# Layer-norm of the second and third token block done channels first, between the evictions of the query/key/value stage

## The chip, the cores and the metric

The kernel runs on one core of a Trainium2 chip. The metric is the device time of one execution in microseconds; the runs before the change have a median of 2848.19. A core has five engines that work side by side, each through its own queue in order: TensorE (PE in the profile; its weight loads are PEld), VectorE (DVE), ScalarE (ACT), GpSimd (POOL) and SyncE (SP), which here issues nearly all DMA transfers. Matmul results stand in PSUM banks until VectorE or ScalarE copies them out, which is called an eviction.

## The reference

The input is an image of 48 x 48 tokens with 768 channels, in fp32. Layer 0 is a transformer block: layer-norm of each token, queries, keys and values from one weight matrix, attention over all 2304 tokens with 12 heads and relative positions in two directions, a projection, a second layer-norm and an MLP with GELU. Layer 1 mixes frequencies: a two-dimensional FFT, a small two-layer network on blocks of 96 channels, an inverse FFT, and the input added. The change touches only the beginning:

```
mu = jnp.mean(x, axis=-1, keepdims=True)
var = jnp.var(x, axis=-1, keepdims=True)
xn = (x - mu) * jax.lax.rsqrt(var + LN_EPS) * g + b
qkv = xn.reshape(B, H * W, C) @ qkv_w + qkv_b
```

## The kernel before

The query/key/value stage takes the tokens in three blocks of 768. TensorE multiplies over the partition axis, so the normalised tokens must stand channels first: `xt`, six chunks of 128 channels by 768 tokens. A block is worked off in nine *units*: six `queries_and_keys` (each for 128 channels of the queries and 128 of the keys) and three `values` (each for two groups of 128 tokens). The order of units is written out in `orders`: block one has the six pairs and then the three values, block two the three values first, block three one pair, the values, five pairs.

A unit is a two-by-two Strassen scheme, so it has seven products instead of eight (`seven`, line 420). A product is three matmuls of 128x128 by 128x384 in fp32, and the profile records each matmul twice. The scheme needs sums of weights and sums of tokens. The sums of weights are made by GpSimd: `left` (lines 159 to 162), for each pair in `weights_of` and once for the values in `weights_of_values`. The sums of tokens are made by VectorE: `sums_of_tokens` (line 177), four operations of 1152 elements for a block; the last one works in place. The seven products go to four PSUM banks, m0 to m3, in the order m0, m1, m2, m3, m0, m2, m3. ScalarE copies the first (line 429), VectorE makes `u` and `u7` of the second and third (431, 433), and four outputs `o` are evicted (460 and 462, or 490 and 492 for values) and stored by SP from seven buffers. A bank is written again only after it has been read.

The tokens of a block come with two `arrive` calls of three tiles of 128 tokens, tokens first. `normal` normalises a tile in place: two `bn_stats`, one `bn_aggr`, a square root on ScalarE, a reciprocal, and one operation of 128x768 (lines 119 to 129). At the beginning of a block `channels_first` turns the six tiles: 36 transposes on TensorE (line 408), into the same banks m0 to m3, evicted with gain and offset by VectorE (411) and ScalarE (415), each six times. Then `sums_of_tokens`, then the first unit. Blocks share one `xt` and one `xs`, in the buffer `main`, and so a block can be turned only when the block before has been multiplied.

Weights of a pair have two slots; after a unit has used a slot, `weights_of` loads the weights for the unit after the next one, and GpSimd makes their sums.

What sets the order: TensorE and SP run in the order of the code (`tc.manual_schedule`, line 545). In this stage the queues of VectorE, ScalarE and GpSimd are ordered by a scheduler, which may, for instance, put the statistics of a tile between two evictions. From the attention on VectorE and ScalarE follow the code too. The buffer `shared` (8064 columns) holds the first head pair's queries, keys and values from block three on; before that it only takes the raw selection constants. After the last unit the relative positions `relative(0, 2)` use TensorE (294), ScalarE (238, 239) and VectorE (240), and then the attention begins with scores (562).

Of the kernel before, what the change touches and what calls it, by code (L numbers as in the profile page):

```python
# [46 lines left out]
def block_then_afno(  # L47
# [3 lines left out]
    x_blocks,  # L51
    qkv_w,
# [50 lines left out]
    oT = dram.tile([C, T], F32, name="oT")  # L103
    den_d = dram.tile([NC * (T // G), 2 * G], F32, name="den_d")
# [88 lines left out]
    with ExitStack() as flag_scope:  # L193
# [12 lines left out]
        with ExitStack() as att:  # L206
# [110 lines left out]
            def constants():  # L317
                nc.vector.memset(relT, 0.0)
                for j in range(2):
                    nc.sync.dma_start(out=relT[ts(j, 64), j], in_=rel)  # L320
                nc.vector.tensor_scalar(relT, relT, HD**0.5, None, ALU.mult)
                raw = shared[:, ds(3 * T + 2 * G, 2 * P)].rearrange("p (a k) -> p a k", a=2)
                for j in range(2):
                    nc.sync.dma_start(out=raw[ts(j, 64)], in_=c_select)
                nc.vector.tensor_copy(select, raw)

            def queries_keys_values(qkv):
# [14 lines left out]
                xt, xs = view(NC, TB), view(3, 3, G)  # L342
# [58 lines left out]

                def channels_first(g):
                    x3 = arrived[g]
# [35 lines left out]
                def queries_and_keys(p, pr, w, ws):  # L439
                    b11, b21, t3, b22, t1, t2, t4 = parts_of_tokens(xt, xs)  # L440
# [15 lines left out]
                    for i, j, bank, other in seven(product):  # L456
# [8 lines left out]
                        )  # L465

                def values(p, i):

                    b11, b21, t3, b22, t1, t2, t4 = parts_of_tokens(xt, xs, ts(i, P))
# [17 lines left out]
                    for k, j, bank, other in seven(product):  # L487
# [6 lines left out]
                        nc.sync.dma_start(out=v_d[ts(t, P), ts(k - 1, CH)], in_=o)  # L494

# [18 lines left out]
                for p in range(T // TB):  # L514
                    for g in (2 * p, 2 * p + 1):
                        channels_first(g)
                    sums_of_tokens(xt, xs)
                    for n, (kind, i) in enumerate(orders[p]):
                        if kind:
                            values(p, i)  # L520
                        else:
                            queries_and_keys(p, i, *ahead.pop(0))
                            if pairs_left:
                                ahead.append(weights_of(pairs_left.pop(0), slot % 2))
                                slot += 1

                        if p == 0 and n in (3, 4):
                            weights_of_values(n - 3)
                        elif (p, n) == (0, 5):
                            constants()  # L530
                        elif p < 2 and n in (1, 2):
                            arrive(2 * p + 1 + n)
                        if p < 2 and 2 <= n < 8:
                            normal(6 * p + 4 + n)
# [7 lines left out]
                        elif p == 2 and n == 5:  # L542
                            fetch_values(0)

# [1175 lines left out]
```

## Time and profile before

| what | value |
|---|---|
| median of three runs | 2848.19 us (2845.54 to 2848.93) |
| the profiled execution, its own time | 2846.82 us |
| its span, first to last instruction | 2844.9 us |
| TensorE busy in the span | 2794.3 us, 98% |
| first product of block one | 21.25 us |
| transposes of block two, of block three begin | 147.13 us, 275.29 us |
| first score product of the attention | 418.75 us |
| granted TensorE clock | 0.999 |

In the lines of a profile a name such as L408 is a line of the kernel, `out<-in` names what an instruction writes and reads, `x18` says how many equal instructions stand together, and what is in brackets is the idle time of the engine before it and the instruction that ended it. In the timeline the first two numbers are start and length in microseconds. SPq is the queue of DMA issues. A group of instructions has its sum and the mean of one in nanoseconds.

### The profile page before, as it was taken

The page shows a single profiled execution, that of the slowest core. Times are in us where ns is not written, and L with a number is a line of the kernel's source. Part 1 is how long each engine was busy: PE and PEld are TensorE (multiplying, and loading weights), DVE is VectorE, ACT ScalarE, POOL GpSimd, SP SyncE. Part 2 cuts the span into 40 slices and gives each one's busy share as a digit, 9 for nine tenths or more (in the row PEclk, how much of TensorE's full clock was granted, in tenths as well). Part 3 has the DMA queues.
Part 4 walks back from the last instruction along what each step waited for, and adds up shares of the span by engine and source line. Part 5 has one row for each costly group of instructions (what it writes and reads, how often), then busy time and mean ns, then how long its engine had stood idle before and what let it go on. Part 6 is the DMA issues. An engine that isn't in the chain of part 4 may idle for free. (4 is left out here: it accounts for less than half of the span.)

```text
span 2844.9 us, 41192 instructions
## 1 busy us (share of the span) xinstructions
PE 2794.3 (98%) x15829; PEld 1722.6 (61%) x15829; DVE 1699.3 (60%) x2540; ACT 920.4 (32%) x1474; POOL 643.5 (23%) x650
## 2 busy tenths in 40 slices
PE   8999999999999999999999999999999999999998
PEld 4555655656566656565555555555555555556887
DVE  5343327676767676666656766675565565566666
ACT  1011116656566566665601211031011211102332
POOL 2303110000000000000064333432333422322433
PEclk9999999999999999999999999999999999999999
DMA  4423275374573736545242121121121212123254
GB/s 146 136 100 111 92 163 110 62 134 83 82 141 54 133 63 110 123 69 97 78 178 78 50 67 45 66 96 51 53 67 45 100 56 67 45 65 112 62 160 143
DMA packets 216493, 262.78 MB, mean 92 GB/s; under 512 B 24524, under 2 KB 196908, under 8 KB 214752
## 3 DMA queue, kind: packets, MB, share of 16 engines
q1 hardware_dynamic: 213784, 258.03, 36.6%
q8 instruction: 127, 2.08, 0.3%
q10 hardware_dynamic: 2440, 1.84, 0.2%
q14 instruction: 78, 0.64, 0.1%
q0 software_dynamic: 64, 0.20, 0.0%
HBM read 143.96 MB, written 52.31 MB: 69 GB/s over the span
## 5 line engine op out<-in xcount | busy, mean ns | idle before, releaser
L581 ACT ACTIVATE main<-sp 128x768 f32<-128x768 f32 x648 | 516.5, 812 | 34.0 <-PE sp L571 19.3
L725 DVE TENSOR_TENSOR pairs<-pairs,main 128x1536 f32<-128x1536 f32 x252 | 443.1, 1758 | 27.2 <-DVE pairs L725 0.9
L571 PE MATMUL sp<-terms,select 64*128 64x384 f32 x1296 | 412.2, 629 | 0.0
L1245 DVE TENSOR_TENSOR main<-o,main 128x384 f32<-128x384 f32 x540 | 299.0, 556 | 38.5 <-PE o L1243 0.3
L1183 PE MATMUL h<-shared,w 128*128 128x384 f32 x864 | 296.6, 486 | 0.7 <-POOL w2s L165 0.7
L562 PE MATMUL sp<-shared 64*128 64x384 f32 x1296 | 265.3, 485 | 2.8 <-DVE o L462 2.2
L562 PE MATMUL sp<-qT,kT 64*128 64x384 f32 x1296 | 264.0, 484 | 0.0
L451 PE MATMUL m<-main 128*128 128x384 f32 x756 | 246.3, 487 | 3.2 <-DVE main L177 2.6
L1183 PEld LDWEIGHTS h<-shared,w 128*128 128x128 f32 x864 | 163.9, 190 | 116.2 <-POOL w2s L165 1.3
L1183 PE MATMUL h<-shared,w1s 128*128 128x384 f32 x648 | 226.7, 486 | 0.0
L627 POOL TENSOR_TENSOR inverse<-inverse,rden 24x32 f32<-24x32 f32 x36 | 15.2, 421 | 927.1 <-DVE sums L626 836.5
L594 PE MATMUL op<-main,shared 128*64 128x384 f32 x1296 | 217.4, 488 | 0.0
L1189 ACT ACTIVATE hT<-c,vec 128x384 f32<-128x384 f32 x108 | 66.5, 615 | 464.5 <-DVE c L1195 464.5
L594 PE MATMUL op<-main,v 128*64 128x384 f32 x1296 | 216.4, 488 | 0.0
L725 DVE TENSOR_TENSOR pairs<-main 128x1536 f32<-128x1536 f32 x36 | 63.3, 1758 | 247.1 <-ACT main L581 247.1
L451 PEld LDWEIGHTS m<-main 128*128 128x128 f32 x756 | 143.1, 190 | 104.0 <-issue 4.9
L1195 DVE TENSOR_TENSOR c<-h,u 128x384 f32<-128x384 f32 x108 | 60.2, 557 | 212.4 <-PE h L1183 212.4
L1243 PE MATMUL o<-w2s,hs 128*128 128x384 f32 x432 | 174.9, 487 | 2.0 <-DVE hs L160 2.0
L1243 PE MATMUL o<-w,hT 128*128 128x384 f32 x432 | 174.9, 486 | 1.9 <-DVE mv L123 1.5
L571 PEld LDWEIGHTS sp<-terms,select 64*128 64x128 f32 x1296 | 125.5, 186 | 83.6
L1183 PEld LDWEIGHTS h<-shared,w1s 128*128 128x128 f32 x648 | 123.1, 190 | 85.9
L165 POOL TENSOR_TENSOR w2s<-w 128x384 f32<-128x384 f32 x36 | 36.0, 1000 | 566.2 <-DMA w<-in_mlp_w_dram 350.1
(187 smaller groups left out, 3995.2 us busy)
## 6 DMA issues: line engine op xcount, KB each, us to landing
w<-in_mlp_w_dram SPq DMA_DIRECT2D x72, 768.0 KB
terms<-col_parts SPq DMA_DIRECT2D x432, 72.0 KB
terms<-row_hi SPq DMA_DIRECT2D x216, 72.0 KB
terms<-row_lo SPq DMA_DIRECT2D x216, 72.0 KB
main<-in_qkv_w_dram SPq DMA_DIRECT2D x36, 384.0 KB
z<-zt SPq DMA_DIRECT2D x48, 192.0 KB
x<-in_x_blocks_dram SPq DMA_DIRECT2D x18, 384.0 KB
k_d<-o SPq DMA_DIRECT2D x36, 192.0 KB
```

The costliest lines, as they stand in the source:

```text
L165: eng.tensor_tensor(t[0], b12, b11, ALU.subtract)
L451: nc.tensor.matmul(bank, a[:, c, :], b[:, c, :], start=(first and c == 0), stop=(c == 2), skip_group_check=not first,)
L562: nc.tensor.matmul(sp[:, j, :G], kT[at, ts(kt, P)], qT[at, ts(c, G)], start=first, stop=not first,)
L571: nc.tensor.matmul(sp[:, j, :G], select[at, a % 2], ready[pr, c][at, a // 2, b], start=first, stop=not first,)
L581: nc.scalar.activation(p, sp[:, :, :G], AF.Exp, scale=HD**-0.5)
L594: nc.tensor.matmul(op[ts(j, 64)], v[:, kt, ts(j, 64)], exps[:, kt, j, :], start=(kt == 0), stop=(kt == NT - 1),)
L725: nc.vector.tensor_tensor(pairs, so_far, exps[:, ds(kt - 1, 2)], ALU.add)
L1183: nc.tensor.matmul(bank[i], a[:, c, :], b[:, c, :], start=(start and c == 0), stop=(c == 2), skip_group_check=not start,)
L1189: nc.scalar.activation(h[:, i, ts(k, G)], src, AF.Gelu, bias=col(V_B1 + 2 * n + i))
L1195: nc.vector.tensor_tensor(t, src, other, ALU.add)
L1243: nc.tensor.matmul(bank[k], a, b, start=start, stop=True, skip_group_check=not start)
L1245: nc.vector.tensor_tensor(dst, bank[k], dst, ALU.add)
```

## The change

The tokens of blocks two and three get to `xt` in another way. They are still loaded tokens first, but only to measure them: `measured` makes mean and variance of a tile, three tiles after the third and three after the fourth unit of the block before. `gathered` makes the reciprocal standard deviation of all six tiles at once, `written` turns the twelve columns of statistics with one transpose into rows and writes them to DRAM, and `spread_out` reads them back into all 128 partitions. The same tokens are loaded a second time channels first (`brought`, from a new input `x_turned`, which is laid out on the host like the others). Then, in the units six to nine of the block before, one small operation after each of the four output evictions (`next_hook`) normalises the new block: `centred` on GpSimd subtracts the mean of a chunk of 128 channels, `scaled` on VectorE multiplies by gain and reciprocal deviation, with the offset added on ScalarE, and `token_sum` makes the four sums of tokens in the ninth unit.

Block two stands in `shared` (`apart`), blocks one and three in `main`. Block one is done as before. From the first unit to the end of the stage VectorE, ScalarE and GpSimd now follow the order of the code too (`part_by_part`). The weights of the values are loaded one unit earlier, and `constants` is split in two steps.

```diff
@@ queries_keys_values @@
-                xt, xs = view(NC, TB), view(3, 3, G)
+                apart = xt, xs
+                tokens = [(view(NC, TB), view(3, 3, G)), apart]
+                tokens.append(tokens[0])
...
+                def gathered(p):
+                    st = ln1.tile([P, 2, 6], F32, name="st", bufs=2)
+                    nc.scalar.activation(st[:, 1], stats[p][:, 1], AF.Sqrt, bias=eps)
+                    nc.vector.reciprocal(st[:, 1], st[:, 1])
+                    nc.vector.tensor_copy(st[:, 0], stats[p][:, 0])
+                    stats[p] = st
+                def written(p):
+                    bank = small_bank()
+                    nc.tensor.transpose(
+                        bank[:12, :P], stats[p].rearrange("p k t -> p (k t)"), ident
+                    )
+                    rows = ln1.tile([12, P], F32, name="stat_rows", bufs=1)
+                    nc.scalar.copy(rows, bank[:12, :P])
+                    nc.sync.dma_start(out=stat_d[p], in_=rows)
+                def measured(t):
+                    p, i = divmod(t, 6)
...
+                    for k in range(2):
+                        nc.vector.bn_stats(parts[:, k, :], src[:, ts(k, C // 2)])
+                    nc.vector.bn_aggr(stats[p][:, :, i], parts.rearrange("p a b -> p (a b)"))
+                def brought(p):
+                    for i in range(2):
+                        nc.sync.dma_start(
+                            out=tokens[p][0][:, ds(3 * i, 3)],
+                            in_=x_turned[ds(i * CH, CH), ts(p, TB)].rearrange(
+                                "(c p) t -> p c t", p=P
+                            ),
+                        )
+                def spread_out(p):
+                    spread[p] = ln1.tile([P, 2, TB], F32, name="stat_all", bufs=1)
+                    nc.sync.dma_start(
+                        out=spread[p].rearrange("p k t -> p (k t)"),
+                        in_=stat_d[p].rearrange("k t -> (k t)").partition_broadcast(P),
+                    )
+                def centred(p, c):
+                    a = tokens[p][0][:, c]
+                    nc.gpsimd.tensor_tensor(a, a, spread[p][:, 0], ALU.subtract)
+                def scaled(p, c):
+                    a = tokens[p][0][:, c]
+                    nc.vector.scalar_tensor_tensor(
+                        a, a, col(V_LN1G + c), spread[p][:, 1], ALU.mult, ALU.mult
+                    )
+                    nc.scalar.activation(a, a, AF.Identity, bias=col(V_LN1B + c))
+                def token_sum(p, i):
...
+                    nc.vector.tensor_tensor(dst, a, b, ALU.subtract)
+                hooks = []
+                def next_hook():
+                    if hooks:
+                        hooks.pop(0)()
@@ queries_and_keys, values: after the store of each output o @@
+                        next_hook()
@@ the loop over blocks @@
-                    for g in (2 * p, 2 * p + 1):
-                        channels_first(g)
-                    sums_of_tokens(xt, xs)
+                    if p == 0:
+                        for g in range(2):
+                            channels_first(g)
+                        sums_of_tokens(*tokens[0])
+                    part_by_part = ExitStack()
+                    part_by_part.enter_context(
+                        tc.manual_schedule(
+                            engines={
+                                mybir.EngineType.DVE, mybir.EngineType.Activation,
+                                mybir.EngineType.Pool,
+                            }
+                        )
+                    )
                     for n, (kind, i) in enumerate(orders[p]):
+                        if p < 2:
+                            q = p + 1
+                            if n in (5, 6):
+                                hooks += [partial(centred, q, 3 * (n - 5) + c) for c in range(3)]
+                            if n in (6, 7):
+                                hooks[:0] = [partial(scaled, q, 3 * (n - 6) + c) for c in range(3)]
+                            if n == 8:
+                                hooks += [partial(token_sum, q, j) for j in range(4)]
...
+                        while hooks:
+                            next_hook()
-                        if p == 0 and n in (3, 4):
-                            weights_of_values(n - 3)
-                        elif (p, n) == (0, 5):
-                            constants()
-                        elif p < 2 and n in (1, 2):
+                        if p < 2 and n in (1, 2):
                             arrive(2 * p + 1 + n)
-                        if p < 2 and 2 <= n < 8:
-                            normal(6 * p + 4 + n)
+                        if p == 0 and n in (2, 3):
+                            weights_of_values(n - 2)
+                        elif p == 0 and n in (5, 6):
+                            constants(n - 5)
+                        if p < 2 and n in (2, 3):
+                            for t in range(3):
+                                measured(6 * (p + 1) + 3 * (n - 2) + t)
+                            if n == 3:
+                                gathered(p + 1)
+                        elif p < 2 and n == 4:
+                            brought(p + 1)
+                            written(p + 1)
+                            spread_out(p + 1)
```

## The prediction

> **What bounds the kernel now.** I read the page's first part, then TensorE's timeline over the query/key/value stage (0 to 419 us) and its waits there, then what the other engines and the DMA queue do at the places found.
>
> ```profile
> PE 2794.3 (98%) x15829; PEld 1722.6 (61%) x15829; DVE 1699.3 (60%) x2540; ACT 920.4 (32%) x1474; POOL 643.5 (23%) x650
> ```
>
> TensorE sets the end: in the page's chain of waits it has 44%, no other engine more than 2%. So the change is worth what it takes off TensorE's own queue between 0 and 419 us, less what it makes TensorE wait. The timeline (start, length, engine, line, operation, count):
>
> ```profile
> 104.63 2.10 PE L482 MATMUL m<-wv,main 128*128 128x384 f32 x6
> 107.69 2.20 PE L482 MATMUL m<-wvs,main 128*128 128x384 f32 x6 [0.95 <-POOL wvs L160]
> 110.26 2.20 PE L482 MATMUL m<-wv,main 128*128 128x384 f32 x6 [0.38 <-POOL wv L162]
> ...
> 118.11 2.10 PE L482 MATMUL m<-wvs,main 128*128 128x384 f32 x6
> 120.04 2.10 PE L482 MATMUL m<-wv,main 128*128 128x384 f32 x6
> ...
> 147.13 2.28 PE L408 MATMUL m<-ident,x 128*128 128x128 f32 x18
> 149.85 2.19 PE L408 MATMUL m<-ident,x 128*128 128x128 f32 x18 [0.44 <-DVE main L411]
> 152.49 2.20 PE L482 MATMUL m<-wv,main 128*128 128x384 f32 x6 [0.44 <-DVE main L411]
> 155.21 2.20 PE L482 MATMUL m<-wvs,main 128*128 128x384 f32 x6 [0.52 <-DVE main L177]
> 157.25 2.10 PE L482 MATMUL m<-wv,main 128*128 128x384 f32 x6
> ```
>
> A product (six records) takes 1.935 us from start to start (118.11 to 120.04), a unit of seven 13.55. Three losses show: a first value unit of 15.41 (104.63 to 120.04), waiting for GpSimd's weight sums; 36 transposes between blocks; and a second product late for the token sums (L177). The later part of the same view:
>
> ```profile
> 275.29 2.33 PE L408 MATMUL m<-ident,x 128*128 128x128 f32 x18
> ...
> 280.70 2.20 PE L451 MATMUL m<-main 128*128 128x384 f32 x6 [0.44 <-DVE main L411]
> 284.13 11.94 PE L451 MATMUL m<-main 128*128 128x384 f32 x36 [1.22 <-DVE main L177]
> 295.91 2.10 PE L482 MATMUL m<-wv,main 128*128 128x384 f32 x6
> ...
> 418.75 0.88 PE L562 MATMUL sp<-shared 64*128 64x384 f32 x3 [2.17 <-DVE o L462]
> ```
>
> The last line is attention's first product. All engines just before it:
>
> ```profile
> 417.00 0.48 ACT L239 CAST row_hi<-small 128x384 fp32r<-128x384 f32 x1
> 417.52 0.56 DVE L240 TENSOR_TENSOR row_lo<-shared,row_hi 128x384 fp32r<-128x384 f32 x1 [3.07 <-ACT row_hi L239]
> 417.99 0.61 DVE L462 SCALAR_TENSOR_TENSOR o<-m,vec,u 128x384 f32<-128x384 f32 x1
> ```
>
> The last eviction stands behind row_lo on VectorE, although its product was over near 415.8.
>
> [...] L162 on GpSimd takes 1.00 us alone (229.46), 2.10 beside the sums of L177 (284.80); the four sums take 5.35 us alone (152.35), 7.56 beside GpSimd (280.57). [...] Here wv, issued at 93.78 behind weights that land at 97.64, lands at 102.3. [...] for a write to DRAM followed by its broadcast back the trace has:
>
> ```profile
> 1427.37 0.32 SPq L641 DMA_DIRECT2D den_d<-rden  x1
> ...
> 1431.07 1.09 SPq L654 DMA_DIRECT2D spread<-den_d  x2
> ```
>
> 3.7 us for the write, and 3.4 until its 192 KB feed VectorE at 1434.51.
>
> **Part by part.** Call E5 and E6 the ends of the fifth and sixth unit's products (E5 is 91.08 in block one).
>
> *Removed from TensorE.* Without transposes and late sums block two's third product follows 147.13 by 2 x 1.935, at 151.00; it started at 157.25: 6.25 us. Block three's first unit took 295.91 - 275.29 = 20.62 instead of 13.55: 7.07 us. The token sums move into the ninth unit. Worst case there, beside GpSimd: 1.89 us each, evictions of 0.6 between; the last starts after the last eviction (0.8 after the unit) and ends 2.7 to 3.2 after it; its reader, product three, starts 3.87 after.
>
> *Moved earlier.* wv's halves load one unit earlier; its sums took 10.4 us (102.32 to 112.78). The second half would be issued near 82 and land near 90.5, the sums end near 101, before 104.63: 15.41 - 13.55 = 1.86 us. If they are not ready, nothing is gained here.
>
> *VectorE in written order.* The last eviction now precedes row_lo. In the built program attention's first product then still waits for ACT's row_hi copy, which ends at 417.48: 418.75 - 417.6 = 1.15 us. Bounds: 0 to 1.3.
>
> *Added to TensorE.* Two transposes of 12 columns of statistics. Eighteen take 2.28 us, 0.13 each; with turning around I take 0.25, at most 0.6. Their input is ready some 9 us earlier (end of unit four): -0.5 us.
>
> Sum: 6.25 + 7.07 + 1.86 + 1.15 - 0.5 = **15.8 us**, if nothing new is waited for.
>
> *What is costed at nothing.* VectorE, per block: six statistics of 1.28 us (two 0.537, one 0.202) stand three at a time after units three and four, 3.8 us, where before there were six normalisations. They delay the next unit's first eviction; ACT's m1 copy, behind the square root, moves from 1.9 to 5.4 us after the unit's start, and its bank is wanted at 7.74. Six `scaled` of 768: no such row; a plain sum of 768 takes 0.96 (L729), half the L725 row is 0.88; I take 1.0, 1.45 beside GpSimd. Six evictions of 0.67 and six normalisations of 0.70 go. ACT: six of 768 at 0.81 (L581), for six of 0.67 and six square roots. GpSimd: six `centred` of 768, between 1.00 (384) and 2.61 (1152): 1.8 each. All fit: in windows of 20 us between 80 and 280 VectorE is busy 4 to 12, ACT 1.3 to 5, GpSimd 0 to 16.
>
> The danger is order, since all of these engines now wait in written order. Per block SP issues behind the fifth unit's weights: two loads of 1152 KB, the 6 KB write, and after that write's landing the 768 KB broadcast. Behind it on SP stand the sixth unit's four stores (seven output buffers, so nobody waits) and the next weights, whose time only comes at E6. When does the broadcast land? Weights land at E5+6.6 (97.64). The window from 57 to 59 us, with rows of 3 KB like these, moved 378 GB/s, so 2.36 MB add 6.2: 12.8. The write lands with their tail, say 13.1. Broadcast: 3.4 plus 576 KB more at 378 GB/s, 1.6: **E5+18.1**. If the write overtook the loads: 12.8. If all ran at the 214 GB/s of the window from 92 to 104: 24.5.
>
> What it may cost. Block one: `scaled` 0 stands before the copy of bank m0 on ACT. Broadcast + 1.8 + 1.45 + 0.81 + 0.48 must be over when m0 is wanted, E5+27.1: it may land up to E5+22.6. Block two: behind three `centred` stand the weight sums of the eighth unit. They start at landing + 5.4, lose some 2.2 to VectorE, and the second is wanted by product two at E5+29.0: landing up to E5+19.4. So 1.3 us of cover in block two, 4.5 in block one; beyond it each microsecond costs one. Last, in block two `centred` 4 and 5 stand behind the ninth unit's weight sums (weights at the seventh unit's end + 6.6, sums 4.0, then 2 x 1.8: +14.3); `scaled` 5 and the last eviction end at +16.3, bank m3 is wanted at +19.35: 3 us of cover.
>
> **The rivals.** (1) *All hidden*, 15.8 us gained. The profiled execution took 2846.82, so 2831.0; the median of the runs shown stands 1.37 higher: **2832.4**, with 2829.5 to 2835.5 for the uncertain terms and the runs' spread. For it: the covers above, and nothing in block three that is tied to a clock time, its loads and stores follow its own units. (2) *Transfers slow*: landing at E5+24.5 costs 5.1 in block two and 1.9 in block one; 2839.4, and some 2836 halfway. For it: 1.3 us of cover is thin. Against: only the weights go at short rows. (3) *It doesn't do what it says*: if the last `scaled` slip to the end of the ninth unit, the four sums (5.35 to 7.56 us) stand in the open in both blocks as they do now, less the 1.9 of the first product, some 10 us in all: 2842.5. For it: `scaled` stand three a unit up to the eighth. Against: they end a whole unit before the sums are due. (4) *Slower*: VectorE stands still at `scaled`, evictions queue behind it and TensorE at full banks in both blocks. With L the landing after E5 it costs (L - 19.4) + (L - 22.6), which eats 15.8 at L = 28.9 and makes the kernel 6 us slower at 31.8, 2854. For it: three engines and a DRAM round trip in one chain. Against: the 3.7 and 3.4 us above; L would have to grow by over 10 us.
>
> **How the numbers follow.** Chances: (1) 0.77, (2) 0.13, (3) 0.05, (4) 0.05. Beyond 0.2% (5.7 us) counts as told from no change. (1), (2) and half of (3) are faster: 0.92; same 0.04; slower 0.04. Range: all of (1) with 1 us more below, and (2) up to nearly its slow end: 2828.5 to 2839.
>
> **What would show it.** Right: no transposes of 128x128 after 22 us; blocks two and three beginning without a gap (block two still at 145.3, that is 147.13 less 1.86 and plus 0.13 to 0.25); 13.55 us for every unit of the first two blocks; the first score product near 403; the broadcast landing 17 to 19.5 us after E5. Wrong: TensorE waiting for GpSimd's L160 or L162 in block two's eighth unit, or for m banks with VectorE or ACT as releaser in units seven and eight; or a first value unit still over 15 us.

## The result, and the profile after

The changed kernel takes 2832.02 us (median of four executions, 2831.46 to 2834.65); the kernel before, run beside it on the same chip, 2848.56 us (2845.54 to 2851.0). The ratio is 0.9944 with a 95% interval of 0.9927 to 0.9961, so the change gains 16.5 us (11 to 21 by the interval). The forecast was 2832.4, a gain of 15.8.

The page's first part of the changed kernel:

```profile
PE 2788.5 (98%) x15759; PEld 1716.2 (61%) x15759; DVE 1700.6 (60%) x2520; ACT 920.6 (32%) x1466; POOL 668.7 (24%) x662
```

TensorE has 70 matmul records fewer (72 transposes gone, two small ones come), GpSimd 25 us more, and TensorE still sets the end. Where the time went is seen in TensorE's timeline over the query/key/value stage (start, length, engine, line, operation, count):

```profile
90.96 0.27 PE L418 MATMUL small<-ident,st 128*12 128x128 f32 x1
91.07 13.71 PE L529 MATMUL m<-main 128*128 128x384 f32 x42
104.62 2.10 PE L561 MATMUL m<-wv,main 128*128 128x384 f32 x6
...
118.16 2.10 PE L561 MATMUL m<-wv,main 128*128 128x384 f32 x6
...
145.25 2.10 PE L561 MATMUL m<-wv,shared 128*128 128x384 f32 x6
147.19 2.10 PE L561 MATMUL m<-wvs,shared 128*128 128x384 f32 x6
149.12 2.10 PE L561 MATMUL m<-wv,shared 128*128 128x384 f32 x6
...
213.09 54.35 PE L529 MATMUL m<-shared,main 128*128 128x384 f32 x168
267.27 13.71 PE L529 MATMUL m<-main 128*128 128x384 f32 x42
280.81 2.10 PE L561 MATMUL m<-wv,main 128*128 128x384 f32 x6
...
375.73 25.51 PE L529 MATMUL m<-main 128*128 128x384 f32 x78 [0.29 <-POOL main L162]
401.17 0.93 PE L296 MATMUL small<-shared,relT 128*48 128x48 f32 x32
403.06 0.92 PE L670 MATMUL sp<-shared 64*128 64x384 f32 x4 [0.96 <-ACT row_hi L241]
```

The first value unit takes 13.54 us (104.62 to 118.16) where it took 15.41. Block two starts at 145.25 with products 1.94 apart from the first on, and block three at 267.27 without a gap. Attention's first product comes at 403.06 instead of 418.75, and now waits for ScalarE's `row_hi`. One wait is new: in block three a product stands 0.55 us late for GpSimd (L162, 375.73). Of the variants of the changed kernel below only the one with one more load has that wait too; the others are to be set against 312.10 - 0.55 = **311.55**.

The traces kept of the kernels below begin their first products up to 1.9 us apart (19.65 to 21.56). So the runs below are compared by one stretch: from the end of the fifth unit's products in block one (where the small transpose stands) to attention's first product. It is 418.75 - 91.08 = 327.67 us in the kernel before and 403.06 - 90.96 = **312.10** in the changed one, 15.57 less. The profiled execution of the changed kernel is the slowest of its four, 2834.65: behind the first score it takes 2429.84 us where the kernel before took 2426.15, because the granted clock, the share of its full speed that TensorE was given, was lower around 1480, 1890 and 2816 us, in code that the change doesn't touch (it falls 1.1, 1.4 and 1.2 us behind there; mean clock 0.83, 0.91 and 0.78 in windows of 20 to 25 us there, before 0.93, 1.00 and 0.92).

What the broadcast of the statistics did, in the order of issue (SP) and landing (GpSimd's first `centred`), block one and block two:

```profile
94.52 0.45 SPq L423 DMA_DIRECT2D stat_d<-stat_rows  x1
103.27 0.36 SPq L449 DMA_DIRECT2D stat_all<-stat_d  x1
```

```profile
108.90 5.36 POOL L456 TENSOR_TENSOR shared<-shared,stat_all 128x768 f32<-128x768 f32 x3 [5.86 <-DMA stat_all<-stat_d]
...
231.58 5.34 POOL L456 TENSOR_TENSOR main<-main,stat_all 128x768 f32<-128x768 f32 x3 [8.21 <-DMA stat_all<-stat_d]
```

Counted from the end of the fifth unit (90.96 and 212.98) it lands at 17.9 and 18.6 us; 18.1 was forecast. The write's landing, which lets SP go on, came at 12.3 (forecast 13.1), the broadcast took 5.6 (5.0).

### The profile page after: what moved, and what is told of

The parts are those of the page before. It is cut to its first block, busy times and chain, and to the rows that moved or that the text cites. A ratio compares the mean times of both kernels' runs of the same rounds, so it can differ in the third digit from the quotient of the medians.

```text
span 2832.9 us, 41042 instructions
## 1 busy us (share of the span) xinstructions
PE 2788.5 (98%) x15759; PEld 1716.2 (61%) x15759; DVE 1700.6 (60%) x2520; ACT 920.6 (32%) x1466; POOL 668.7 (24%) x662
## 5 line engine op out<-in xcount | busy, mean ns | idle before, releaser
L689 ACT ACTIVATE main<-sp 128x768 f32<-128x768 f32 x648 | 516.3, 812 | 34.5 <-PE sp L679 19.6
L529 PE MATMUL m<-main 128*128 128x384 f32 x504 | 164.6, 488 | 2.4 <-DVE main L179 1.8
L702 PEld LDWEIGHTS op<-main,v 128*64 128x64 f32 x1296 | 96.9, 137 | 92.7 <-issue 67.7
```

Of the source, the lines that this page charges most:

```text
L529: nc.tensor.matmul(bank, a[:, c, :], b[:, c, :], start=(first and c == 0), stop=(c == 2), skip_group_check=not first,)
L689: nc.scalar.activation(p, sp[:, :, :G], AF.Exp, scale=HD**-0.5)
L702: nc.tensor.matmul(op[ts(j, 64)], v[:, kt, ts(j, 64)], exps[:, kt, j, :], start=(kt == 0), stop=(kt == NT - 1),)
```

## The experiments

My theory: the gain is the work taken off TensorE's queue, the terms add up and are independent of each other, and it stays whole as long as the broadcast lands ahead of the covers (a cover is the latest landing, counted from the end of the fifth unit, that makes TensorE wait for nothing). Rivals: the gain is the written order; the chain is limited by engine load and not by order; the terms hang together; the covers are far larger than I made them, so that the transfers don't matter.

### The cover: one and two loads more ahead of the statistics

One more load of 1152 KB into a spare buffer, ahead of the write, in both blocks; its data is not used.

```diff
                             brought(p + 1)
+                            brought_again(p + 1, 1)
                             written(p + 1)
```

> The changed kernel with one more load of 1152 KB (half of the channels-first tokens once more, into a spare buffer that nobody reads) between the token loads and the write of the statistics. Theory (thin cover): the broadcast lands 3.1 us later (1.18 MB at 378 GB/s), 21.0 and 21.7 us after the fifth unit's end in blocks one and two instead of 17.9 and 18.6. Block one still has cover (22.6): 0 us. Block two is over its cover of 19.4 to 19.7 by 2.0 to 2.3 us, and TensorE waits that long for GpSimd's weight sums (L162 or L164) in the eighth unit. First score product at 405.1 to 405.4 us instead of 403.06; time about 2834. Rival (ample cover: the normalisation has whole units of slack and nobody waits for the landing): 403.1, no wait, 2832.

Measured: 2836.83 us (2834.68 to 2838.75), ratio 0.9955 [0.9939, 0.9972]; the stretch is 315.62, 3.5 more than the changed kernel's (2.0 to 2.3 expected). The broadcast landed at 22.0 and 22.1 us (21.0 and 21.7 expected). TensorE's timeline shows where that was late:

```profile
119.02 2.20 PE L571 MATMUL m<-wv,main 128*128 128x384 f32 x6 [0.42 <-ACT o L579]
...
241.92 2.20 PE L539 MATMUL m<-shared,main 128*128 128x384 f32 x6 [0.61 <-ACT o L548]
245.50 25.73 PE L539 MATMUL m<-shared,main 128*128 128x384 f32 x78 [1.38 <-POOL main L162]
```

GpSimd's weight sums (L162) hold block two's eighth unit, as expected. But ScalarE's copy of bank m0 (L579 and L548, the eviction of a unit's fifth product) holds TensorE too, in both blocks, where the prediction had cover left in block one up to 22.6. VectorE's timeline in block one says why:

```profile
115.09 5.04 DVE L470 SCALAR_TENSOR_TENSOR shared<-shared,vec,stat_all 128x768 f32<-128x768 f32 x2 [1.69 <-POOL shared L466]
```

Two `scaled` beside GpSimd took 5.04 us, 2.5 each, and I had taken 1.45. With ScalarE's offset at 0.94 instead of 0.81 that makes the chain 1.2 us longer, and the cover 21.4 instead of 22.6.

Two more loads (edit as above, with 2; the second spare buffer is one of those that the attention uses later for `terms`).

> As before with two more loads of 1152 KB. Theory (thin cover): landing at 24.1 and 24.8 us after the fifth unit's end; block one 1.5 us over its cover (bank m0 behind ScalarE's offset: TensorE waits for ACT at the start of the eighth unit), block two 5.1 to 5.4 us over (TensorE waits for GpSimd's weight sums). First score product near 409.7 us, time about 2838.6. Rival (ample cover): 403.1 and 2832. A third possibility, that only one of the two covers is right, shows in which block TensorE waits.

Measured: 2842.06 us (2837.79 to 2847.31), ratio 0.9977 [0.9969, 0.9986]; the stretch is 321.25, 9.7 more than 311.55 (6.6 to 6.9 expected). The landing was at 24.4 and 24.0.

```profile
121.26 3.76 PE L574 MATMUL m<-wv,main 128*128 128x384 f32 x6 [2.84 <-ACT o L582]
...
247.58 19.43 PE L542 MATMUL m<-shared,main 128*128 128x384 f32 x54 [2.48 <-ACT o L551]
```

In both blocks the copy of m0 is what TensorE waits for: 3.0 us in block one at a landing of 24.4, which puts the end of the cover at 24.4 - 3.0 = 21.4. Some 3 us of the loss isn't waiting: the product at 121.26 took 3.76 us instead of 2.10. In the same trace a table of stretches (us; busy time of PE, PEld, DVE, ACT and POOL; granted clock; DMA share; GB/s) shows a lower clock around it:

```profile
118.00:122.00 4.00, 1.16 (x3) 0.50 (x2) 4.00 (x2) 1.30 (x2) 4.00 (x3) 0.88 0.75 183
122.00:126.00 4.00, 4.00 (x10) 2.27 (x9) 4.00 (x6) 2.35 (x3) 3.84 (x4) 0.70 0.43 152
```

TensorE had paused, and came back at half clock: 0.12 and 0.30 of 4 us missing are 3.4 us at half. So a microsecond beyond the cover can cost more than one. In block two the slow product also hid the expected wait for GpSimd: L162 was over at 251.1, about when that product was. The rival that the transfers don't matter falls.

### The late chain on ScalarE alone

The kernel with one more load, with ScalarE's offsets written behind the unit's last eviction instead of between its evictions.

```diff
-                    nc.scalar.activation(a, a, AF.Identity, bias=col(V_LN1B + c))
+                    late.append(partial(nc.scalar.activation, a, a, AF.Identity, bias=col(V_LN1B + c)))
...
                         while hooks:
                             next_hook()
+                        while late:
+                            late.pop(0)()
```

> The kernel with one more load (e1) with ScalarE's three offsets of a unit moved behind the unit's evictions, so that the copy of bank m0 no longer stands behind the first of them. e1 measured, from the end of the fifth unit of block one to the first score product, 315.6 us instead of the changed kernel's 312.1: 0.7 lost in block one (TensorE waits for ScalarE), 2.8 in block two (0.6 for ScalarE, then 1.4 for GpSimd's L162). If the chain broadcast, centred 0, scaled 0, offset, copy of m0 is what binds block one, its 0.7 us vanish altogether and ScalarE is no releaser in either block; block two keeps a wait for L162 of 2.0 to 2.6 us, since GpSimd's sums are as late as before: 314.4 to 314.9 us. If the landing itself binds (any order behind it costs the same), 315.6 stays.

Measured: 2834.74 us (2833.33 to 2835.93), ratio 0.9952 [0.9935, 0.9968]; the stretch is 314.23. ScalarE is no longer a releaser anywhere in the stage; one wait is left:

```profile
243.81 25.53 PE L539 MATMUL m<-shared,main 128*128 128x384 f32 x78 [2.12 <-POOL main L162]
```

So the two limits are separate, as the prediction had them: the chain through `scaled` and the offset to m0, and GpSimd's weight sums behind three `centred`. The broadcast landed at 21.9 us in block two and TensorE was 2.3 late, so the cover of the weight sums ends at 19.6, where the prediction had 19.4.

### The statistics written ahead of the loads

```diff
-                            brought(p + 1)
                             written(p + 1)
+                            brought(p + 1)
                             spread_out(p + 1)
```

> The changed kernel with the write of the statistics issued ahead of the two channels-first loads, so that it waits in the queues only behind the weights. Theory (covered): the broadcast is issued some 5 us earlier, but its data still come behind the loads; landing near 15.5 us after the fifth unit's end instead of 17.9 and 18.6, GpSimd starts that much earlier, and TensorE gains nothing: first score product at 403.1 within 0.2 us, time as the changed kernel's. Rival (the landing is on the path even now): up to 2 us earlier.

Measured: 2831.68 us (2830.9 to 2832.17), ratio 0.9939 [0.9923, 0.9956]; the stretch is 311.50, the 311.55 of the kernel without that wait in block three. The SP queue:

```profile
91.69 0.51 SPq L423 DMA_DIRECT2D stat_d<-stat_rows  x1
92.25 0.91 SPq L440 DMA_DIRECT2D shared<-in_x_turned_dram  x2
95.39 0.34 SPq L449 DMA_DIRECT2D stat_all<-stat_d  x1
```

Without the two loads ahead of it the write takes 3.7 us (91.69 to 95.39), as the attention's write did before; behind them it took 8.75 (94.52 to 103.27). With the write first, the broadcast is issued 3.1 us behind the loads and takes 10.0 us (95.39 to 105.40) instead of 5.6 (103.27 to 108.90), and the landing is at 16.1 instead of 17.9. Nothing waits for it, so it buys no time. The median is not told apart from the changed kernel's.

### Order or load: the mean subtracted by VectorE

```diff
-                    nc.gpsimd.tensor_tensor(a, a, spread[p][:, 0], ALU.subtract)
+                    nc.vector.tensor_tensor(a, a, spread[p][:, 0], ALU.subtract)
```

> The changed kernel with the mean subtracted by VectorE instead of GpSimd, at the same places in the code. VectorE now stands at the first subtraction, in the sixth unit, until the broadcast lands. Theory (order, not load): the eviction of m2 behind two subtractions ends near 20.4 us after the fifth unit's end in block one and 21.2 in block two, and the bank is wanted at 17.4: TensorE waits 3.1 and 3.8 us for DVE in the sixth or seventh unit (third product), 6.9 in all; first score product near 410.0 us, time about 2839. Rival (load: VectorE has the 12 us for it, and GpSimd is relieved): 403.1 and 2832, no waits.

Measured: 2842.99 us (2839.14 to 2846.37), ratio 0.9979 [0.9972, 0.9986]; the stretch is 319.79, 8.2 more. VectorE's timeline in block one:

```profile
108.09 1.83 DVE L456 TENSOR_TENSOR shared<-shared,stat_all 128x768 f32<-128x768 f32 x2 [9.32 <-DMA stat_all<-stat_d]
109.84 0.61 DVE L540 SCALAR_TENSOR_TENSOR o<-m,vec,u 128x384 f32<-128x384 f32 x1
```

VectorE idles 9.32 us at the head of its queue, waiting for the broadcast, and an eviction stands behind it. TensorE lost 2.9 us in block one and 3.7 in block two waiting (3.1 and 3.8 expected), and 1.6 more at half clock (granted clock 0.57 from 236 to 240). The trace names no releaser for these two waits; the one in block one ends at 110.55, just behind that eviction (109.84 to 110.45). VectorE was busy for 4.3 of the 20 us from 90 to 110 and for 15.2 of the next 20, so it was not full: what costs is whose queue the waiting instruction stands in. This is the fourth rival's mechanism at work. The change escapes it because the first instruction that waits for the broadcast is on GpSimd.

### Block three, and block two, turned the old way

Block three as before, block two as changed (the other guards are set in the same way):

```diff
-                    if p == 0:
-                        for g in range(2):
+                    if p != 1:
+                        for g in (2 * p, 2 * p + 1):
                             channels_first(g)
...
-                        if p < 2 and n in (2, 3):
+                        if p == 1 and 2 <= n < 8:
+                            normal(10 + n)
+                        if p < 1 and n in (2, 3):
```

> The changed kernel with block three alone done as before: tokens first, normalised tile by tile by VectorE, 36 transposes and the four sums at the block's start; block two as changed. Theory (each block's turn costs what its transposes and late sums took): block three gets its 7.1 us back, so 319.2 us from the end of block one's fifth unit to the first score product instead of 312.1, time about 2839. Rival (most of the gain comes from the written order of the three engines): 312 to 314.

Measured: 2840.03 us (2837.57 to 2841.94), ratio 0.997 [0.9959, 0.9982]; the stretch is 318.41. TensorE in block three has the losses of before again:

```profile
266.18 2.34 PE L486 MATMUL m<-ident,x 128*128 128x128 f32 x18
268.97 2.19 PE L486 MATMUL m<-ident,x 128*128 128x128 f32 x18 [0.44 <-DVE main L489]
271.60 2.20 PE L529 MATMUL m<-main 128*128 128x384 f32 x6 [0.45 <-DVE main L489]
275.03 11.94 PE L529 MATMUL m<-main 128*128 128x384 f32 x36 [1.22 <-DVE main L179]
```

The other way round, block two turned (in its own buffer) and block three as changed:

```diff
-                    if p == 0:
-                        for g in range(2):
+                    if p != 2:
+                        for g in (2 * p, 2 * p + 1):
                             channels_first(g)
-                        sums_of_tokens(*tokens[0])
+                        sums_of_tokens(*tokens[p])
...
-                        if p < 2 and n in (2, 3):
+                        if p == 0 and 2 <= n < 8:
+                            normal(4 + n)
+                        if p == 1 and n in (2, 3):
```

> The changed kernel with block two alone done the old way: normalised tokens first beside block one's units, turned by 36 transposes at its beginning, then the token sums. Block three stays as changed. If the prediction's first term is right, block two's third product comes 6.25 later than in the changed kernel, less the 0.11 of the small transpose that goes: from the end of the fifth unit to attention's first product 318.2 instead of 312.1 (317.7 if the 0.55 that TensorE waits for GpSimd in block three goes too), time near 2838 to 2839. If the two blocks' terms depend on each other, for instance because the second load and the first share something, it lands elsewhere: below 316 or above 320.

Measured: 2839.91 us (2836.91 to 2840.64), ratio 0.9967 [0.9954, 0.9979]; the stretch is 317.62 (its fifth unit ends at 90.35, its first score comes at 407.97).

With the 0.11 of the small transpose that each leaves out, block three's turn is worth 318.41 - 311.55 + 0.11 = 6.97 us (7.07 forecast) and block two's 317.62 - 311.55 + 0.11 = 6.18 (6.25). They don't hang together.

### The token sums at the head of the new block

First trial: the sums taken out of the ninth unit and written at the beginning of the next block's part.

```diff
+                    if p:
+                        sums_of_tokens(*tokens[p])
                     for n, (kind, i) in enumerate(orders[p]):
...
-                            if n == 8:
-                                hooks += [partial(token_sum, q, j) for j in range(4)]
```

> The changed kernel with the four sums of tokens of blocks two and three not in the ninth unit of the block before, but at the new block's start, behind the last eviction. No transposes. They start 0.75 us after the last product and take 1.35 each if GpSimd is idle: product two (wants the second sum) 1.6 us late, product three (wants the fourth) 0.7 more, 2.3 a block, 4.6 in all: 316.7 us from the end of block one's fifth unit to the first score product, with TensorE waiting for DVE; time about 2836.6. Rival (the sums are hidden behind the first product anyway): 312.1.

Measured: 2833.18 us (2831.66 to 2836.25), ratio 0.9948 [0.9932, 0.9965]; the stretch is 312.64, and no product waits for a sum. The 1.1 more than 311.55 lie in block two: 0.7 of waiting for GpSimd's sums in the eighth unit, where the broadcast landed at 19.1, and 0.3 at 263.52 in the ninth, for VectorE's `u7` (L511), which stands behind three of the moved sums (258.32 to 262.3). The expectation missed, and the run didn't test it. VectorE's timeline near the end of block one:

```profile
130.98 0.56 DVE L571 TENSOR_TENSOR o<-m,u 128x384 f32<-128x384 f32 x1 [0.45 <-PE m L561]
131.53 4.02 DVE L179 TENSOR_TENSOR shared<-shared 128x1152 f32<-128x1152 f32 x3
...
144.52 0.56 DVE L571 TENSOR_TENSOR o<-m,u 128x384 f32<-128x384 f32 x1 [1.38 <-PE m L561]
```

Three of the sums run at 131.53, as the ninth unit begins, and the first ran even earlier, at 119.38: ahead of all that VectorE does for the ninth unit, which the code writes before them. The written order binds the instructions of one block; it doesn't tie the next block's behind them, and the sums were placed as soon as their data were there. What the run does say: earlier than between the ninth unit's evictions costs the new block's products nothing, and the ninth unit 0.3 us.

Second trial: the sums inside the block's own order, behind the last eviction.

```diff
                         while hooks:
                             next_hook()
+                        if p < 2 and n == 8:
+                            for j in range(4):
+                                token_sum(p + 1, j)
...
-                            if n == 8:
-                                hooks += [partial(token_sum, q, j) for j in range(4)]
```

> The changed kernel with the four token sums of blocks two and three written behind the last eviction of the block before. If they cost what VectorE's order says: in block two the last eviction ends near 145.9 and the sums start there, 1.37 each, so the second product of the block, which reads the second sum, starts at 148.7 instead of 147.2, 1.5 later; in block three they stand beside GpSimd's weight sums, 1.6 to 2.1 each, and the second product starts 1.6 to 2.8 later. Together 3.1 to 4.3, from block one's small transpose to attention's first product 315.2 to 316.4 instead of 312.1, with VectorE as the releaser of both products. If all four sums stand in the open, as the third rival of the prediction took it: 10 us, near 322. If the place of the sums doesn't matter: 312 to 312.7.

Measured: 2837.94 us (2835.21 to 2839.8), ratio 0.9961 [0.9947, 0.9975]; the stretch is 316.39, 4.8 more.

```profile
149.22 2.20 PE L561 MATMUL m<-wvs,shared 128*128 128x384 f32 x6 [1.37 <-DVE shared L472]
151.88 2.20 PE L561 MATMUL m<-wv,shared 128*128 128x384 f32 x6 [0.46 <-DVE shared L472]
...
273.89 2.17 PE L529 MATMUL m<-main 128*128 128x384 f32 x6 [1.66 <-DVE main L472]
276.50 9.91 PE L529 MATMUL m<-main 128*128 128x384 f32 x30 [0.44 <-issue]
```

The second product of each block waits for the second sum and the third, some 0.7 more, for the third, which the expectation had left out. So the place of the sums is needed, but the third rival's size was wrong by more than half: it took all four sums as standing in the open, 10 us, and only what the second and third product read does, 4.8.

### The value weights one unit later

```diff
-                        if p == 0 and n in (2, 3):
-                            weights_of_values(n - 2)
+                        if p == 0 and n in (3, 4):
+                            weights_of_values(n - 3)
```

> The changed kernel with the weights of the values loaded one unit later, as before the change. Their sums start 10.6 us after the fifth unit's end, the fourth (now last in written order) ends at 21.1 and is wanted at 17.4: TensorE waits 3.7 us for GpSimd in the first value unit, 3.8 in all, twice the 1.86 of the kernel before, where the scheduler had put that sum third. The broadcast, behind 1152 KB more and behind these sums on GpSimd, is covered by that wait. 315.9 us from the end of block one's fifth unit to the first score product, time about 2835.8. Rival (worth what it was before, 1.9): 314.0.

Measured: 2838.14 us (2835.2 to 2840.37), ratio 0.9961 [0.9947, 0.9975]; the stretch is 317.09, 5.5 more.

```profile
107.70 2.20 PE L561 MATMUL m<-wvs,main 128*128 128x384 f32 x6 [0.54 <-POOL wvs L162]
112.95 3.67 PE L561 MATMUL m<-wv,main 128*128 128x384 f32 x6 [3.05 <-POOL wv L164]
```

The third product waits for the last sum, which GpSimd now makes fourth in written order, where the kernel before makes it third. The waiting is what was expected, 4.0 for 3.8; the other 1.6 are again a product at half clock (3.67 instead of 2.10; granted clock 0.57 from 112 to 116).

### The order alone

The kernel before, with its stage in written order for the three engines and nothing else; here only the added context is shown.

```diff
+                    part_by_part.enter_context(
+                        tc.manual_schedule(
+                            engines={
+                                mybir.EngineType.DVE, mybir.EngineType.Activation,
+                                mybir.EngineType.Pool,
+                            }
+                        )
+                    )
```

> The kernel before with nothing but the written order for VectorE, ScalarE and GpSimd, as the changed kernel has it: transposes, normalisation and loads as before. If the gain of the change comes from the work taken off TensorE, this is no gain: the last eviction goes ahead of row_lo (1.15 less), the sums of the value weights keep their place behind the others on GpSimd (up to 2.6 more): from the start of the fifth unit's end to attention's first product 326.5 to 330.3 where the kernel before has 327.7, time 2847 to 2851. If the order alone were what helps: 320 or less, time below 2841.

Measured: 2849.55 us (2847.13 to 2853.77) beside 2848.93, ratio 1.0004 [0.9997, 1.0011]; the stretch is 329.74 (its fifth unit ends at 90.05, its first score comes at 419.79). The rival that the written order is the gain falls. Inside the stretch the order does both: it gains 1.2 us at attention's first product and 0.6 at block three's token sums, and loses 3.8 in the first value unit, where TensorE waits 3.06 us for the last weight sum, now made fourth, and half clock follows (granted clock 0.67 from 111.5 to 115 and 0.84 to 118.5). The changed kernel escapes that loss by loading these weights earlier.

The opposite: the changed kernel with block three left to the scheduler.

```diff
-                    part_by_part.enter_context(
-                        tc.manual_schedule(
...
+                    if p < 2:
+                        part_by_part.enter_context(
+                            tc.manual_schedule(
```

> The changed kernel with block three's order on VectorE, ScalarE and GpSimd left to the scheduler, as before; row_lo stands ahead of the last eviction again. If the fourth term of the sum is right, attention's first product comes 1.15 later, 313.2 behind block one's small transpose instead of 312.1, with VectorE's last eviction as its releaser instead of ACT's row_hi. If the 0.3 to 0.5 that TensorE waits in block three's first weights for GpSimd go away with the written order, 312.7 to 312.9. If that order is worth nothing: 312.1.

Measured: 2835.08 us (2834.6 to 2836.76), ratio 0.9955 [0.9938, 0.9972]; the stretch is 313.30, 1.75 more.

```profile
399.22 0.93 PE L296 MATMUL small<-shared,relT 128*48 128x48 f32 x32
402.32 0.88 PE L671 MATMUL sp<-shared 64*128 64x384 f32 x3 [2.17 <-DVE o L540]
```

From the last small matmul to the first score it is 3.10 us, as before the change, and 1.89 in the changed kernel (401.17 to 403.06): 1.21 us for the eviction ahead of `row_lo`. The other 0.55 arose in block two. TensorE's products show no wait there, but its weight loads (PEld) do:

```profile
240.31 1.59 PEld L529 LDWEIGHTS m<-shared,main 128*128 128x128 f32 x6 [0.59 <-POOL main L162]
242.34 13.20 PEld L529 LDWEIGHTS m<-shared,main 128*128 128x128 f32 x42 [0.43 <-POOL main L164]
256.14 3.85 PEld L529 LDWEIGHTS m<-shared,main 128*128 128x128 f32 x13 [0.61 <-issue]
```

The first two wait for GpSimd's weight sums in the eighth unit: the broadcast landed at 19.8 us here, just beyond that cover. The third, in the ninth unit, begins just behind an eviction (255.47 to 256.08) that had to wait for a `scaled` of 2.55 us. So this part belongs to block two, where the broadcast landed later, and not to the order in block three. The median is 3 us above the changed kernel's. The half clock that followed the 2.17 us pause here (0.53 over the next 3.4 us) is part of that: attention's fifth score product starts 5.0 us after the first, where in the kernel before it is 4.25.

## Why the prediction was right

Each term of the sum, as forecast and as measured. "In the changed kernel" compares the two traces; "undone alone" is the experiment that takes back that part only.

| term | forecast | in the changed kernel | undone alone |
|---|---|---|---|
| block two's turn and late sums | 6.25 | 6.25 | 6.18 |
| block three's turn and late sums | 7.07 | 7.08 | 6.97 |
| sums of the value weights earlier | 1.86 | 1.87 | not tried as it was |
| last eviction ahead of `row_lo` | 1.15 | 1.21 | 1.21 |
| two small transposes | -0.5 | -0.22 | |
| something new waited for (0.55 of it in block three) | 0 | -0.6 | |
| sum | 15.8 | 15.6 | |

How the third column comes out: block two's third product stands 58.16 us after the fifth unit's end (149.12 - 90.96) and stood 66.17 before (157.25 - 91.08). The 8.01 between are the value weights' 15.41 - 13.54 = 1.87 and block two's 6.25, less one small transpose of 0.11. Block three's first unit takes 280.81 - 267.27 = 13.54 instead of 20.62. From there to the first score it is 122.25 instead of 122.84: 1.21 from the eviction, less 0.62, of which 0.55 is the wait at 375.73.

**Removed work.** Right to a tenth. It could be, because each loss was a gap in TensorE's own timeline with a product step of 1.935 us beside it, so nothing had to be guessed.

**Small transposes.** 0.11 each, where I took 0.25: TensorE goes from them to the next product (90.96 to 91.07) without the turning round that I allowed for. (The sign "block two still at 145.3" comes to 145.4 to 145.5 by the sum that stands beside it; it began at 145.25.)

**The landing.** 17.9 and 18.6 for 18.1. The working held, its parts less well than their sum: in block one the write landed 0.8 earlier than forecast and the broadcast took 0.6 longer, which nearly cancels. That the write lands with the loads' tail was not seen directly; with a third load ahead of it the write took 12.2 us instead of 8.75.

**The covers.** Here a step was mis-sized. The prediction's chain "broadcast + 1.8 + 1.45 + 0.81 + 0.48" left 22.6 us in block one. `scaled` beside GpSimd measures 2.5 in the run with one more load and up to 2.6 in the changed kernel (the first one of block one 2.0, the first one of block two 2.6), and 1.0 when alone:

```profile
113.03 3.72 DVE L460 SCALAR_TENSOR_TENSOR shared<-shared,vec,stat_all 128x768 f32<-128x768 f32 x2
...
126.58 1.94 DVE L460 SCALAR_TENSOR_TENSOR shared<-shared,vec,stat_all 128x768 f32<-128x768 f32 x2
...
253.44 2.54 DVE L460 SCALAR_TENSOR_TENSOR main<-main,vec,stat_all 128x768 f32<-128x768 f32 x1 [3.62 <-POOL main L456]
```

The first and the last line are beside GpSimd, the middle one is not. The last line began with a `centred` of 1.8 us on GpSimd (253.4 to 255.2) and ended 0.8 us after it: 2.54 for an operation that takes 1.0 alone, so 1.45 was no upper bound. The true cover is 21.3 to 21.4 at this chain, in both blocks. The forecast didn't fall over it, since the landing came 3 us ahead. In block two GpSimd's weight sums were ready at 240.28 and 242.91 (forecast need 242.12 and 244.05), so 1.1 to 1.8 us to spare, where the prediction had 1.3.

**The new wait.** I named block two's eighth unit as the place to look for GpSimd's sums. The one wait that came is in block three, where I had written that nothing is tied to a clock time. It is 0.55 us, and absent in ten of the eleven variants. The SP queue and GpSimd's show where it comes from:

```profile
367.16 1.12 SPq L374 DMA_DIRECT2D main<-in_qkv_w_dram  x2
```

```profile
373.41 1.00 POOL L161 TENSOR_TENSOR main<-main 128x384 f32<-128x384 f32 x1 [15.11 <-PE small L296]
```

The load of that unit's weights stands on SP behind 24 loads of `terms` and four stores, and was issued 6.1 us before the unit began (373.24); GpSimd's first sum began 0.2 us behind the unit. With one more load it was 6.4 and 0.1 us behind, with the same wait. In the other ten variants GpSimd's first sum began 0.3 to 2.4 us ahead of the unit. So block three does hang on a transfer's time, which the prediction had ruled out; why these weights came later in two of the runs stays open.

**The rivals.** Slow transfers (2839.4) and the slower case (2854) rested on a landing at 24.5 and beyond. With two loads more it landed at 24.4 and 24.0, for which the prediction's covers give (24.4 - 22.6) + (24.0 - 19.4) = 6.4 us; the cost was 9.7. Block one cost 4.7, priced at 1.8: its cover ends earlier, and half clock comes on top. Block two cost 5.1, priced at 4.6. So the point from which the change makes the kernel slower should lie nearer than the 28.9 that I gave; that is argued and wasn't tried.

**Chances and range.** All of the range above 2835.5 stood for a landing that didn't come late. That was a fair reading of 1.3 us of cover; the runs show that it would have been used up by one more load in the queue.

**What was luck.** The two medians agree to 0.4 us, far closer than the interval can tell, and the stretch itself gained 15.6. Two misses of opposite sign stand in that sum, transposes 0.3 cheaper and waits of 0.6 that were not foreseen. The chain that was mis-sized by 1.2 us had 4.5 us of cover in the forecast, so that miss could not show.

## What to carry to other kernels

Read a change in preparatory work from the gaps in the limiting engine's timeline, and then ask of every new instruction that waits for a transfer whose queue it stands in: the same twelve subtractions cost nothing on GpSimd, where each takes 1.8 us, and 8.2 us in all on VectorE, where each takes 0.9 but stands ahead of evictions. Price an operation that stands beside another engine by the longest time measured there, not by an average: `scaled` took 1.0 us alone and up to 2.6 beside GpSimd, where I had taken 1.45. And order written for one part of a kernel need not bind the next part: look at the built order before you trust an experiment that moves work across such a border.

## What the runs showed of the hardware that was not expected

A pause of TensorE can cost more than itself. After idle times of 2.17 (free order), 2.48 and 2.84 (two loads more), 3.05 (value weights later), 3.06 (order alone) and 3.52 us (mean on VectorE, block two) it ran at half clock for some 3.4 us, from about a microsecond after its return at the latest; after 2.12 (late offsets), 2.17 (kernel before, first score) and 2.76 us (mean on VectorE, block one) it did not. The stretches of the run with the mean on VectorE, block one and block two (columns as above):

```profile
110.00:114.00 4.00, 3.45 (x11) 2.16 (x12) 3.25 (x6) 0.00 (x0) 0.00 (x0) 1.00 0.34 110
...
236.00:240.00 4.00, 3.68 (x7) 2.15 (x8) 2.08 (x4) 0.00 (x0) 0.00 (x0) 0.57 0.39 121
```

The half clock costs about 1.6 us each time in this stage (3.76 or 3.67 for a product of 2.10). The idle time alone doesn't decide it: 2.17 us were enough in one place of this stage and not in another, and in a later stage of the changed kernel 1.62 us were enough, before a product at 1889.36 (granted clock 0.63 from 1890.3 to 1893 and 0.76 to 1896, again 3.4 us at half; 0.50 in each microsecond from 1891 to 1894). What does decide it was not shown.
